# Eight row scatters per block: one burst, or one per round behind the newest matmul

## The chip, the cores and the metric

The kernel runs on one core of one Trainium2 chip. The metric is the device time of one execution in microseconds. The kernel before was run three times without the profiler: 1150.1, 1150.43 and 1151.41 us, so the median is 1150.43 us. One more execution was recorded by the profiler. A core has four compute engines with a queue of instructions each: PE (matrix multiply), DVE (vector), ACT (activations), POOL (GpSimd); SP only issues DMAs here. Each queue is worked off in order, and engines wait for each other through semaphores.

## The reference, cut to what matters

A pre-norm block over 4 sequences of 2048 tokens, width 256, float32: causal linear attention with 16 heads, then a mixture of 8 experts, two experts for each token.

```
x = x + linear_attention(layernorm(x))        # elu(q)+1, elu(k)+1, running sums over the sequence
h = layernorm(x)
logits = h @ router_w.T                       # 8 experts
top2, idx = top_k(logits, 2); p = softmax(top2)
x = x + sum over the two experts e of p_e * (gelu(h @ w1[e] + b1[e]) @ w2[e] + b2[e])
```

The reference works out every expert for every token and weights with zeros. The kernel computes only the chosen pairs, so it has to sort tokens by expert: that is what the scatters are for.

## The kernel before, in words

The 8192 tokens are 16 blocks of 512. A block passes through three stages in three successive steps of the outer loop (line 907): `stage_a` (norm, q, k, v, prefix sums), `stage_b` (scores and values, 128 tokens at a time) and `stage_c` (output projection, second norm, router, places of the tokens). In step s the loop runs `stage_a(s)`, `stage_b(s - 1)` and `stage_c(s - 2)` side by side. They are Python generators: one round of the inner loop (lines 926 to 933) advances each of them to its next `yield`, which writes its instructions down.

`stage_c` ends with the routing: DVE works out for each of the 512 tokens, and for each of its two experts, a row number in a table `rows` in DRAM in which each expert has a region (`slots`, line 616). Then eight indirect DMAs on POOL's queue (line 620; two experts by four groups of 128 tokens) write the normalised token with its weights there, one row of 1040 bytes per token. Before the change all eight are written down in one piece of `stage_c`, in its fourth round, so they stand one behind the other in POOL's queue.

The expert part works on tiles of 256 rows of one expert (`slot_tiles`, line 728; 68 tiles). SP fetches the rows of a tile three tiles ahead (`fetch_rows`, line 734), first-layer weights two ahead (`fetch_in`), second-layer weights and bias one ahead (`fetch_out`). A fetch of rows waits for every scatter written down so far (`after(i, writes + cleared)`, line 747). PE transposes the rows (`turned`, line 776), multiplies by the first weights (`hidden`, ph, line 804), ACT applies gelu (line 810), PE multiplies by the second weights (`output`, py, line 821), DVE adds bias and weights the rows (y, lines 826 and 830), and two indirect DMAs on POOL add the tile to the output (`store`, line 835), each pair after the pair before it has landed. Tiles can be worked on while later blocks are still in attention: as soon as a round of tiles is known to be full (`ROUND_ENDS`), the inner loop mixes steps of that work (two per tile) between the rounds of the stages. How early in a step they come is set by one number per kind of step:

```
order = (20, 12, 5)[(s > NBLK - 1) + (s > NBLK)]
...
        i += 1
        while ran < share and ran * order < i * share:
            work.step()
            ran += 1
```

A planner of the framework then orders each engine's list; only SP's is kept as written. POOL has, besides scatters and adds, one addition of the output bias per block (`x`, line 319).

Of the kernel before, what the change touches and what calls it, by code (L numbers as in the profile page):

```python
# [24 lines left out]
def kernel(  # L25
# [41 lines left out]
    nc = tc.nc  # L67
# [241 lines left out]

    made = {}  # L310
    zlast = [None]

    entered = {}

# [9 lines left out]
    def stage_a(n: int):  # L324
        b, s0 = blocks[n]
        if n not in entered:
            enter(n)
            yield
        xt, xn = entered.pop(n)
        if n + 1 < len(blocks):  # L330
            xs[n + 1] = load_x(n + 1)
        xnT = att.tile([P, NCC, TB], F32, tag="xnT", name=f"xnT_{n}")
        transposed(xn, xnT, "xn")
        yield
        qT = att.tile([P, NCC, TB], F32, tag="qT", name=f"qT_{n}")
        kT = att.tile([P, NCC, TB], F32, tag="kT", bufs=2, name=f"kT_{n}")
        for w, bias, dst in ((wk_sb, bk_sb, kT), (wq_sb, bq_sb, qT)):
            for m in range(NCC):
                pp = bank([P, TB], "pp")
                for cc in range(NCC):  # L340
                    nc.tensor.matmul(  # L341
                        pp, w[:, cc, ts(m, P)], xnT[:, cc, :],
                        start=(cc == 0), stop=(cc == NCC - 1),
                    )
                elu1(pp, bias[:, m : m + 1], dst[:, m, :])
            yield

        z = att.tile([P, NCC, TB], F32, tag="z", name=f"z_{n}")
        carry = small.tile([P, NCC], F32, tag="carry", name=f"carry_{n}")
        for m in range(NCC):  # L350
            nc.vector.tensor_tensor_scan(
                z[:, m, :], kT[:, m, :], kT[:, m, :],
                0.0 if s0 == 0 else zlast[0][:, m : m + 1], ALU.add, ALU.bypass,
            )
        nc.vector.tensor_copy(carry, z[:, :, TB - 1])
        zlast[0] = carry
        nc.vector.tensor_tensor(z, z, qT, ALU.mult)
        vp = vpads[n % 2]
        vp_v = vp.rearrange("p t q (s d) -> p t q s d", s=4)[:, :, :, 0::3, :]
        for t2 in range(NT // 2):  # L360
            pv = bank([P, 2, D], "pv")
            for j in range(2):
                for cc in range(NCC):
                    nc.tensor.matmul(  # L364
                        pv[:, j, :], xnT[:, cc, ts(2 * t2 + j, P)], wv_sb[:, cc, :],
                        start=(cc == 0), stop=(cc == NCC - 1),
                    )
            for j in range(2):
                nc.vector.tensor_tensor(
                    vp_v[:, 2 * t2 + j],  # L370
                    pv[:, j, :].rearrange("p (q s d) -> p q s d", s=2, d=HD),
                    bv_bc.rearrange("p (q s d) -> p q s d", s=2, d=HD),
                    ALU.add,
                )
        yield
        k_tok = att.tile([P, NT, D], F32, tag="k_tok", bufs=2, name=f"k_tok_{n}")
        for t2 in range(NT // 2):
            pk = bank([P, 2, D], "pk")
            for j in range(2):
                for m in range(NCC):  # L380
                    nc.tensor.transpose(  # L381
                        pk[:, j, ts(m, P)], kT[:, m, ts(2 * t2 + j, P)], ident
                    )
            nc.scalar.copy(k_tok[:, 2 * t2 : 2 * t2 + 2, :], pk)
        if n < ROUND_ENDS[0] + 2:

            enter(n + 1)
        yield

        pd = bank([P, P], "pd")  # L390
        for m in range(NCC):
            for t in range(NT):
                nc.tensor.matmul(
                    pd[W * t : W * t + W, :], heads[:, m, :], z[:, m, ts(t, P)],
                    start=(m == 0), stop=(m == NCC - 1), skip_group_check=True,
                    tile_position=(0, W * t),
                )
        rden = small.tile([P, P], F32, tag="rden", name="rden")
        nc.vector.tensor_scalar_add(rden, pd, DEN_EPS)
        nc.vector.reciprocal(rden, rden)  # L400
        yield
        qs = att.tile([P, NCC, TB], F32, tag="qs", bufs=2, name=f"qs_{n}")
        prs = [bank([P, NCC, P], f"pr_{t}") for t in range(NT)]
        for m in range(NCC):
            for t in range(NT):
                part = slice(W * t, W * t + W)
                nc.tensor.matmul(
                    prs[t][:, m, :], spread[part, m], rden[part, :], start=True, stop=True,
                    tile_position=(W * t, 0),
                )  # L410
        for t in range(NT):
            nc.vector.tensor_tensor(
                qs[:, :, ts(t, P)], qT[:, :, ts(t, P)], prs[t], ALU.mult
            )
        made[n] = (xt, kT, qs, k_tok, vp, vp_v)
        yield
# [4 lines left out]
    def stage_b(n: int):  # L421
# [35 lines left out]
        for c in range(NT):  # L457
            nxt = scores(c + 1) if c + 1 < NT else None
            yield
            st = sstate[0]  # L460
            pn = bank([P, NCC, P], "pn")
            for m in range(NCC):
                for g in range(NG):
                    part = slice(W * g, W * g + W)
                    nc.tensor.matmul(  # L465
                        pn[part, m, :], st[part, m], qs[part, m, ts(c, P)],
                        start=(m == 0), stop=False, skip_group_check=True,
                        tile_position=(W * g, W * g),
                    )
            for m in range(NCC):  # L470
                for par in range(2):
                    for g in range(NG):
                        nc.tensor.matmul(  # L473
                            pn[W * g : W * g + W, m, :],
                            vp[:, c, NG * m + g, W * par : W * par + W],
                            at[:, g, m, par, :],
                            start=False, stop=(par == 1), skip_group_check=True,
                            tile_position=(0, W * g),
                        )
            nc.scalar.copy(vT[:, :, ts(c, P)], pn)  # L480
            if s0 + (c + 1) * P < S:
                for m in range(NCC):
                    for g in range(NG):
                        nc.tensor.matmul(
                            state_ps[W * g : W * g + W, m],
                            k_tok[:, c, P * m + W * g : P * m + W * g + W],
                            vp_v[:, c, NG * m + g],
                            start=(s0 == 0 and c == 0 and m == 0), stop=True,
                            skip_group_check=True, tile_position=(0, W * g),
                        )  # L490
                st = small.tile([P, NCC, 2, HD], F32, tag="S", bufs=2, name=f"S_{n}_{c}")
                nc.vector.tensor_tensor(
                    st, state_ps, own2.unsqueeze(1).to_broadcast([P, NCC, 2, HD]), ALU.mult
                )
                sstate[0] = st
            at = nxt
            yield
# [13 lines left out]
    def stage_c(n: int):  # L511
# [103 lines left out]
        slots = small.tile([P, M], U32, tag="slots", name="slots")  # L615
        nc.vector.tensor_copy(slots, slot_f)
        nc.vector.tensor_copy(ends[:, :, 0], upto[:, :, M])
        for k in range(2):
            for t in range(NT):
                s = ins_of(nc.gpsimd.indirect_dma_start(  # L620
                    out=rows[:, :],
                    out_offset=bass.IndirectOffsetOnAxis(
# [3 lines left out]
                ))  # L626
                apart(s, "rows")
                after(s, cleared)
                writes.append(s)
        yield  # L630

# [96 lines left out]
    def slot_tiles(todo):  # L728
# [67 lines left out]
        def hidden(j):  # L796
            xT, w1t, bias = (state[j][key] for key in ("xs", "w1", "bias"))
            hT = moe.tile([P, NFC, ST], F32, tag="hT", name="hT")
            for f2 in range(NFC // 2):
                ph = bank([P, 2, ST], "ph")  # L800
                for i in range(2):
                    f = 2 * f2 + i
                    for cc in range(NCC):
                        nc.tensor.matmul(  # L804
                            ph[:, i, :], w1t[:, cc, ts(f, P)], xT[:, cc, :],
                            start=(cc == 0), stop=(cc == NCC - 1),
                        )
                for i in range(2):
                    f = 2 * f2 + i
                    nc.scalar.activation(  # L810
# [4 lines left out]
        def output(j):  # L815
# [2 lines left out]
            py = bank([P, NS, D], "py")  # L818
            for a in range(NS):
                for f in range(NFC):  # L820
                    nc.tensor.matmul(  # L821
                        py[:, a, :], hT[:, f, ts(a, P)], w2t[:, f, :],
                        start=(f == 0), stop=(f == NFC - 1),
                    )
            yt = moe.tile([P, NS, D], F32, tag="y", bufs=4, name=f"y_{j}")
            nc.vector.tensor_tensor(  # L826
                yt, py, b2t.unsqueeze(1).to_broadcast([P, NS, D]), ALU.add
# [79 lines left out]
    for s in range(NBLK + 2):  # L907
# [13 lines left out]
            left = max(0, left - 2 * HOLD)  # L921
        share = -(-left // (upto - s + 1))
        ran = 0
        order = (20, 12, 5)[(s > NBLK - 1) + (s > NBLK)]
        i = 0
        while gens:
            for it in list(gens):
# [64 lines left out]
```

## Time and profile before

| | us |
|---|---|
| median of three runs | 1150.43 |
| the profiled execution, its own time | 1243.11 |
| its span, first to last instruction | 1241.1 |
| PE busy in the span | 1088.4 |
| DVE busy | 750.7 |
| ACT busy | 414.0 |
| POOL busy | 389.1 |
| mean granted PE clock, share of full speed | 0.931 |

The profiled execution takes 92.7 us more than the median of the runs without the profiler. In a row of groups the columns are line, engine, operation, what it writes and reads, count, then busy time and the mean of one, then the engine's idle time ahead of them and who ended it. In a row of the timeline they are start, duration, engine, line, operation, names, count, and in brackets the idle time of the engine and what ended it; "issue" means that the profile shows nothing that the engine waited for, and "remote" that the release came with no recorded instruction at its time. In a table by windows each row gives a stretch, its length, and for each engine the busy time and the number of instructions, then the granted PE clock, the share of the DMA engines and GB/s.

By stretches the span divides so: up to 70 us the start; to about 225 us blocks in attention alone; to 420 us the first expert tiles among them; from 420 to 898 us seven steps of the loop that look alike, with four tiles each; to about 1020 us the last two steps; then 25 tiles alone until PE ends at 1217.4 us; and 23.7 us in which the last output adds land.

### The profile page before, as it was taken

Reading aid. Unit: us, or ns where it says so; the run is one execution under the profiler, and the core shown is the slowest. Engines: PE = TensorE matmul, PEld = TensorE weight load, DVE = VectorE, ACT = ScalarE, POOL = GpSimd, SP = SyncE. Lnnn points to the kernel's source line nnn. Section 1 sums busy time; section 2 is a strip of 40 time slices with the busy share of each in tenths; the row PEclk is TensorE's granted clock in tenths of the full one; section 3 lists DMA queues with packets and bytes.
Section 4 is the critical chain, followed back from the end, with each engine's and each line's share of the span. In section 5 each row is a group of like instructions: output and inputs, shape, how many; then the busy total and the mean of one; then the engine's idle time right before and its main releaser. Section 6 shows DMA issues by size and latency. Waiting matters only on the chain.

```text
span 1241.1 us, 25308 instructions
## 1 busy us (share of the span) xinstructions
PE 1088.4 (88%) x9504; PEld 835.7 (67%) x9504; DVE 750.7 (60%) x2535; ACT 414.0 (33%) x824; POOL 389.1 (31%) x302
## 2 busy tenths in 40 slices
PE   4987777888888999899998999998999969999992
PEld 2655544565757677676776776776768748888881
DVE  8775856667576857675674848674676455333330
ACT  3442322424242525344352625253343112222220
POOL 4002113021313342324233242423242424444444
PEclk9888877888888999999998999899999979999996
DMA  5011111523323446172636364451726348898873
GB/s 188 2 35 41 42 51 42 162 92 81 112 69 112 124 107 184 50 214 63 195 76 184 95 169 122 123 151 46 202 62 184 96 133 258 234 232 229 238 169 39
DMA packets 128732, 155.37 MB, mean 125 GB/s; under 512 B 9952, under 2 KB 105952, under 8 KB 128608
## 3 DMA queue, kind: packets, MB, share of 16 engines
q1 hardware_dynamic: 84944, 101.78, 26.1%
q0 software_dynamic: 25728, 34.88, 15.3%
q10 hardware_dynamic: 17936, 17.07, 4.3%
q8 instruction: 76, 1.25, 0.4%
q14 instruction: 48, 0.39, 0.1%
HBM read 108.05 MB, written 45.65 MB: 124 GB/s over the span
## 4 chain that ended last, share of the span: by engine, by line
PE 67%; DVE 23%; issue 4%; DMA 2%; another core or an unknown queue 2%; ACT 1%; ACTq 0%; POOL 0%; DVEq 0%; POOLq 0%
PE py L821 19%; PE ph L804 16%; PE pp L341 7%; PE pn L473 6%; DVE at L447 5%; DVE st L269 3%; PE pv L364 3%; PE pn L465 3%; PE sc L442 3%; PE pt_xn L262 2%; DMA out_dram<-y,to 2%; PE pt_xs L776 2%; DVE x L524 2%; PE pk L381 1%
## 5 line engine op out<-in xcount | busy, mean ns | idle before, releaser
L835 POOL DMA_INDIRECT out_dram<-y,to x136 | 217.6, 1600 | 513.2 <-DVE y L830 329.4
L821 PE MATMUL py<-w,hT 128*128 128x256 f32 x1088 | 263.3, 395 | 4.8 <-issue 4.8
L804 PE MATMUL ph<-xT,w 128*128 128x256 f32 x1088 | 254.0, 386 | 2.2 <-issue 1.4
L821 PEld LDWEIGHTS py<-w,hT 128*128 128x128 f32 x1088 | 209.5, 198 | 44.4 <-issue 15.6
L804 PEld LDWEIGHTS ph<-xT,w 128*128 128x128 f32 x1088 | 207.6, 193 | 33.9 <-issue 4.4
L810 ACT ACTIVATE hT<-ph,b1t 128x256 f32<-128x256 f32 x272 | 114.0, 470 | 344.2 <-PE ph L804 288.7
L447 DVE TENSOR_TENSOR at<-sc,causal 128x512 f32<-128x512 f32 x256 | 160.4, 683 | 21.0 <-PE sc L442 14.9
L826 DVE TENSOR_TENSOR y<-py,b 128x512 f32<-128x512 f32 x68 | 47.0, 690 | 197.7 <-PE py L821 186.7
L620 POOL DMA_INDIRECT rows<-xn,slots x128 | 124.2, 970 | 84.8 <-issue 83.0
L777 DVE COPY xT<-pt_xs 128x512 f32<-128x512 f32 x68 | 46.9, 690 | 120.5 <-PE pt_xs L776 97.1
L319 POOL TENSOR_TENSOR x<-x,bo_bc 128x1024 f32<-128x1024 f32 x16 | 39.2, 2449 | 248.0 <-ACT xn L293 97.8
L473 PE MATMUL pn<-at,vpad 128*32 128x128 f32 x2048 | 92.3, 301 | 15.7 <-issue 15.3
L473 PEld LDWEIGHTS pn<-at,vpad 128*32 128x32 f32 x2048 | 62.7, 119 | 37.7 <-issue 36.9
L433 ACT ACTIVATE qM<-qs,parity 128x256 f32<-128x256 f32 x128 | 57.0, 499 | 91.5 <-issue 35.2
L262 PE MATMUL pt_xn<-ident,xn 128*128 128x128 f32 x256 | 47.3, 328 | 44.8 <-DVE xn L298 43.4
L480 ACT COPY vT<-pn 128x256 f32<-128x256 f32 x64 | 23.6, 368 | 176.2 <-PE pn L473 84.9
L442 PE MATMUL sc<-qM,kT 32*128 32x256 f32 x1024 | 75.7, 405 | 0.7 <-DVE xT L777 0.7
L262 PEld LDWEIGHTS pt_xn<-ident,xn 128*128 128x128 f32 x256 | 35.7, 168 | 56.9 <-issue 34.6
L442 PEld LDWEIGHTS sc<-qM,kT 32*128 32x128 f32 x1024 | 47.5, 187 | 27.1 <-issue 17.5
L341 PE MATMUL pp<-xnT,wq_sb 128*128 128x512 f32 x128 | 62.3, 627 | 0.0
L341 PE MATMUL pp<-xnT,wk_sb 128*128 128x512 f32 x128 | 59.8, 611 | 0.2 <-ACT xnT L263 0.2
L519 PE MATMUL px<-wo_sb,vT 128*128 128x256 f32 x256 | 59.4, 385 | 0.0
(152 smaller groups left out, 1375.2 us busy)
## 6 DMA issues: line engine op xcount, KB each, us to landing
w<-in_w_dram SPq DMA_DIRECT2D x136, 512.0 KB
xs<-rows SPq DMA_DIRECT2D x68, 260.0 KB
b<-in_b_dram SPq DMA_DIRECT2D x68, 128.0 KB
out_dram<-x ACTq DMA_DIRECT2D x16, 512.0 KB
x<-in_x_dram ACTq DMA_DIRECT2D x15, 512.0 KB
rows<-none SPq DMA_DIRECT2D x1, 2340.0 KB
out_dram<-y,to POOLq DMA_INDIRECT x136
rows<-xn,slots POOLq DMA_INDIRECT x128
```

Of the source, the lines that this page charges most:

```text
L262: nc.tensor.transpose(pt[:, t, :], src[:, t, ts(cc, P)], ident)
L341: nc.tensor.matmul(pp, w[:, cc, ts(m, P)], xnT[:, cc, :], start=(cc == 0), stop=(cc == NCC - 1),)
L433: nc.scalar.activation(qM[:, :, par, :], qs[:, :, ts(c, P)], AF.Copy, scale=parity[:, par : par + 1],)
L442: nc.tensor.matmul(sc[g][:, m, :, :], kT[part, m, ts(c, P)], qM[part, m, :, :], start=True, stop=True,)
L447: nc.vector.tensor_tensor(at[:, g].rearrange("p m r i -> p (m r) i"), sc[g].rearrange("p m r i -> p (m r) i"), causal.unsqueeze(1).to_broa ...
L473: nc.tensor.matmul(pn[W * g : W * g + W, m, :], vp[:, c, NG * m + g, W * par : W * par + W], at[:, g, m, par, :], start=False, stop=(par = ...
L519: nc.tensor.matmul(px[:, j, :], vT[:, cc, ts(2 * t2 + j, P)], wo_sb[:, cc, :], start=(cc == 0), stop=(cc == NCC - 1),)
L620: s = ins_of(nc.gpsimd.indirect_dma_start(out=rows[:, :], out_offset=bass.IndirectOffsetOnAxis(ap=slots[:, 2 * t + k : 2 * t + k + 1], axi ...
L804: nc.tensor.matmul(ph[:, i, :], w1t[:, cc, ts(f, P)], xT[:, cc, :], start=(cc == 0), stop=(cc == NCC - 1),)
L810: nc.scalar.activation(hT[:, f, :], ph[:, i, :], AF.Gelu, bias=bias[:, f : f + 1])
L821: nc.tensor.matmul(py[:, a, :], hT[:, f, ts(a, P)], w2t[:, f, :], start=(f == 0), stop=(f == NFC - 1),)
L835: i = ins_of(nc.gpsimd.indirect_dma_start(out=out_rows, in_=yt[:, a, :], in_offset=None, compute_op=ALU.add, bounds_check=T - 1, oob_is_er ...
```

## The change

Block n's scatters are spread over rounds: from the second on, each is preceded by a `yield` of `stage_c`, and each of the eight is made to wait on a semaphore for the matmul that was written down last among those of six places: pk, pd, pn of the attention, ph and py of the tiles, each now passed through `issued`. The last block keeps its scatters together. `stage_c` has seven rounds more for that, and `order` is raised from 20 to 27 and from 12 to 19 for the steps concerned.

```
+    latest = []
+
+    def issued(i):
+        latest[:] = [ins_of(i)]
...
-                        nc.tensor.matmul(
+                        issued(nc.tensor.matmul(
                             pn[W * g : W * g + W, m, :],
...
-                        )
+                        ))
...
+        spread_out = n < len(blocks) - 1
         for k in range(2):
             for t in range(NT):
+                if spread_out and (k or t):
+                    yield
                 s = ins_of(nc.gpsimd.indirect_dma_start(
...
                 apart(s, "rows")
                 after(s, cleared)
+                if spread_out:
+                    after(s, latest)
                 writes.append(s)
...
-        order = (20, 12, 5)[(s > NBLK - 1) + (s > NBLK)]
+        order = (27, 19, 5)[(s > NBLK - 1) + (s > NBLK)]
```

The same wrapping in `issued` is made at pk (line 381), pd (393), ph (804) and py (821).

More of the change, by code (lines that the diff above doesn't have):

```diff
@@ L380, in stage_a @@
                 for m in range(NCC):
-                    nc.tensor.transpose(
+                    issued(nc.tensor.transpose(
                         pk[:, j, ts(m, P)], kT[:, m, ts(2 * t2 + j, P)], ident
-                    )
+                    ))
             nc.scalar.copy(k_tok[:, 2 * t2 : 2 * t2 + 2, :], pk)
@@ L396, in stage_a @@
                     tile_position=(0, W * t),
-                )
+                ))
         rden = small.tile([P, P], F32, tag="rden", name="rden")
@@ L472, in stage_b @@
                     for g in range(NG):
-                        nc.tensor.matmul(
+                        issued(nc.tensor.matmul(
                             pn[W * g : W * g + W, m, :],
@@ L478, in stage_b @@
                             tile_position=(0, W * g),
-                        )
+                        ))
             nc.scalar.copy(vT[:, :, ts(c, P)], pn)
@@ L803, in hidden @@
                     for cc in range(NCC):
-                        nc.tensor.matmul(
+                        issued(nc.tensor.matmul(
                             ph[:, i, :], w1t[:, cc, ts(f, P)], xT[:, cc, :],
                             start=(cc == 0), stop=(cc == NCC - 1),
-                        )
+                        ))
                 for i in range(2):
@@ L820, in output @@
                 for f in range(NFC):
-                    nc.tensor.matmul(
+                    issued(nc.tensor.matmul(
                         py[:, a, :], hT[:, f, ts(a, P)], w2t[:, f, :],
                         start=(f == 0), stop=(f == NFC - 1),
-                    )
+                    ))
             yt = moe.tile([P, NS, D], F32, tag="y", bufs=4, name=f"y_{j}")
```

## The prediction

> **What bounds the kernel now.** I read the page first, for the span, the engines and the scatters' group.
>
> ```profile
> span 1241.1 us, 25308 instructions
> ...
> PE 1088.4 (88%) x9504; PEld 835.7 (67%) x9504; DVE 750.7 (60%) x2535; ACT 414.0 (33%) x824; POOL 389.1 (31%) x302
> ...
> L620 POOL DMA_INDIRECT rows<-xn,slots x128 | 124.2, 970 | 84.8 <-issue 83.0
> ```
>
> PE is the bound; POOL is busy for 31% and the chain of waits gives it 0%. So the change can pay only where scatters hold up PE. The windows of one of the seven like steps (the part ahead of block 10's eight scatters, the scatters, the part behind) show whether they do:
>
> ```profile
> 693.89:718.63 24.74, 24.48 (x197) 17.68 (x196) 18.01 (x51) 12.11 (x20) 8.93 (x5) 1.00 0.24 44
> 718.63:729.97 11.34, 8.94 (x79) 5.93 (x78) 1.05 (x4) 1.44 (x4) 7.71 (x8) 1.00 0.36 108
> 729.97:760.68 30.71, 29.63 (x300) 24.06 (x300) 23.04 (x83) 13.69 (x30) 6.92 (x5) 1.00 0.77 219
> ```
>
> PE (first pair) is full ahead and behind, and idles 2.4 of 11.34 us during the scatters. The timeline of PE shows that it loses more than idle time:
>
> ```profile
> 721.02 1.47 PE L473 MATMUL pn<-at,vpad 128*32 128x128 f32 x31
> 722.84 0.27 PE L473 MATMUL pn<-at,vpad 128*32 128x128 f32 x1 [0.35 <-issue]
> 723.04 0.82 PE L381 MATMUL pk<-ident,kT 128*128 128x128 f32 x4
> 724.31 0.54 PE L381 MATMUL pk<-ident,kT 128*128 128x128 f32 x3 [0.45 <-issue]
> 725.02 0.27 PE L381 MATMUL pk<-ident,kT 128*128 128x128 f32 x1 [0.17 <-issue]
> 725.73 1.12 PE L821 MATMUL py<-w,hT 128*128 128x256 f32 x4 [0.45 <-issue]
> 727.15 1.24 PE L821 MATMUL py<-w,hT 128*128 128x256 f32 x5 [0.30 <-issue]
> 728.59 0.91 PE L821 MATMUL py<-w,hT 128*128 128x256 f32 x3 [0.20 <-issue]
> 730.00 1.02 PE L821 MATMUL py<-w,hT 128*128 128x256 f32 x4 [0.50 <-issue]
> 730.96 0.50 PE L442 MATMUL sc<-qM,kT 32*128 32x256 f32 x4
> ```
>
> From start to next start, pn takes 2.02 us, pk 2.69, py 5.23, with pauses for which the profile names no cause. Undisturbed, the same groups look like this (the step of block 8's scatters):
>
> ```profile
> 599.92 1.08 PE L473 MATMUL pn<-at,vpad 128*32 128x128 f32 x32
> 600.82 0.31 PE L484 MATMUL state_ps<-vpad,k_tok 128*32 128x32 f32 x16
> ...
> 603.41 3.72 PE L821 MATMUL py<-w,hT 128*128 128x256 f32 x16
> 607.07 1.15 PE L442 MATMUL sc<-qM,kT 32*128 32x256 f32 x16
> ```
>
> There pn takes 0.90 and py 3.66; pk's eight transposes take about 0.96, as eight of the same shape (pt_xn) do. So this burst costs PE 1.1 + 1.7 + 1.6 = 4.4 us. Last, who waits:
>
> ```profile
> ACT vT L480 <- remote: 81.2, 9, 9.4
> ...
> SPq L743 <- DMA rows<-xn,slots: 125.0, 16, 49.5
> ```
>
> Nine times ACT's copy of pn starts up to 9.4 us after pn's last record, when a burst ends[...].
>
> **The change part by part.**
>
> *The bursts removed.* I summed PE's time beyond the undisturbed time of what it ran, from first scatter to 1.5 us after the last, over all sixteen bursts: 91 us; 73 us if each window is set against one of equal length ahead of it (early blocks wait on DVE anyway). If that were all real it would be 6 to 8% of the median. But these numbers belong to a recorded execution, and that one takes 1243.11 us, 92.7 more than the median of 1150.43. The 92.7 us have to lie somewhere in this trace. They are not in the 25 tiles at the end (PE busy 173.00 of the 173 us from 1038 on), nor in the like steps outside bursts (PE is busy 64.35 of 68.4 us on the mean of six of them, and the rest lies mostly in the bursts). Taking the bursts out gives 1243 - 91 = 1152, almost the median. Nothing else of that size is there.
>
> [...] in the burst of block 15 (from 1019.71 us, the same eight scatters) PE runs only the long ph and py and loses at most 1.5 us; in the other bursts it has just sent pn, 32 matmuls in 0.9 us. [...] By the rows alone the burst is worth 73 to 91 us[...]. I take 0 us and keep 0 to -75 (15 of 16 bursts change) as ends.
>
> *The clock.* [...] In the burst at 581.19 the granted clock falls to 0.5 for 3.4 us[...]. But py takes 5.33 us there, and 5.23 us in the burst above at clock 1.00: the measurement decides, and the clock is charged nothing of its own.
>
> *The waits.* 120 scatters wait for a matmul. It is older in the program than anything queued behind them: in POOL's list of the changed kernel, from block 6 on, the order is 2 scatters, adds of a tile, 3 scatters, adds, 3 scatters, adds, then the bias addition. An add needs a later py, so it would have waited anyway; four y buffers and 12 to 17 us per tile cover some us of lateness. The bias addition is needed two steps later. Cost 0; without that cover, a late add would hold DVE's y, then PE.
>
> *SP.* Its list is unchanged, but fetches of rows now wait for two or three scatters, several times per step, not once for eight. Today one such fetch stands until 593.15 us, right after a burst; its rows are transposed near 615, and the first-layer weights queued behind it (593.72) are used at 611.70: 18 us of cover. A group of three scatters is 3.8 us of POOL plus landing. Cost 0 while a fetch is held less than about 15 us longer than today.
>
> *The number 27.* This moves work on every engine. Instruction counts are equal but for ACT, with 14 table loads less (1.28 us each, 18 us, off the path: ACT is busy 33%). PE's list has the same instructions in another order from block 5 on. In the like steps, tiles' ph and py now stand one by one between short attention groups. I followed each short group to what it waits for. Undisturbed there is little to win: per step sc to pt_xn2 stands 1.0 us for the second norm and 0.4 us in pt_xn2; plt 0.3. In the changed order PE has the same work between px and pt_xn2, but DVE's norm no longer has a tile's copy (0.69 us) and small operations in front: perhaps 0.5 to 1 us per step. Near the end, ph 41 moves between pn and px, where PE stood 1.2 us. Against it: in block 5's step only sc (1.1 us) now lies between pd and pr, whose reciprocal needs about 1.3 us, and the router's pc of two steps lies 4.6 us behind plt, not 8. Ten steps at -0.6, -1 at the end, +1 early: -6 us, bounds +3 and -10.
>
> Sum against the recorded execution: 1243 less 55 to 75 us of bursts, about 1170 to 1185. Against the median: 1150.4 - 6 = 1144.5.
>
> **The rivals.**
>
> *The bursts are real without the profiler as well* (12%). For it: nothing in the trace names the recorder. Against: the 92.7 us would then need another home. A quarter of the 75 us gives about 1130, all 1075.
>
> *Nothing gained from the order* (13%): the norm chain stands just as long, about 1150.
>
> *Slower, through SP* (28%): a fetch of rows waits for scatters that wait for a matmul that waits for DVE; behind it the weights of the next tile queue up. It decides when a fetch is held over 15 us longer than today; beyond that each us late is a us of PE. The 49.5 us longest wait of that kind speaks for it, the 18 us of cover against. One us in each of ten steps, without the gain of the order: 1160; half of it, 1155.
>
> **How the numbers follow.** Likeliest (47%) is the order's gain alone: 1144.5, its own range 1141 to 1149. What a measurement of this kernel can tell from no change is about 0.2%, 2.3 us. Of the 47%, 9 end within that; with the 13% of the second rival, same is 22%; faster 38 + 12 = 50%; slower 28%. The range leaves out the lower half of the first rival and the far end of the third: 1124 to 1160.
>
> **What would show it.** Right: the recorded execution falls by 55 us or more while the median moves by less than 1%; pn, pk and py near scatters back at 0.9, 1.0 and 3.6 us; "remote" gone from ACT's waits; PE full in the steps. Wrong: a median 20 us or more lower (the bursts were real), or SP's waits on scatters grown with PE waiting for ph or pt_xs (the third rival). If single scatters still stop PE, the recorded execution hardly falls.

## The result and the profile after

The changed kernel takes 1183.88 us (median of 6 runs, 1175.12 to 1191.05) against 1150.92 us (6 runs, 1150.1 to 1152.77) for the kernel before: 1.028 times as long, 95% interval 1.0258 to 1.0301. The prediction was 1144.5 us, 1124 to 1160: wrong in sign, and outside its range. The profiled execution of after is its fastest, 1175.12 us. Its page, with the span, the busy times and the scatters' group:

```profile
span 1173.4 us, 25336 instructions
...
PE 1046.8 (89%) x9504; PEld 810.5 (69%) x9504; DVE 752.6 (64%) x2535; ACT 395.2 (34%) x810; POOL 386.5 (33%) x302
...
L628 POOL DMA_INDIRECT rows<-xn,slots x128 | 125.5, 980 | 299.7 <-PE pv L368 87.2
```

POOL's idle time ahead of the scatters has grown from 84.8 to 299.7 us and is now owed mostly to PE (226.8 us of it): the change does what it says. PE's busy time must not be set against the 1088.4 us of before, which belong to an execution of 1243 us. A second recorded execution of the kernel before (experiment 1) is the one to compare with: span 1148.3 us, PE busy 1035.8.

The timeline of PE around the second group of state products (`state_ps`) in a like step shows where the time goes. After:

```profile
442.04 0.31 PE L488 MATMUL state_ps<-vpad,k_tok 128*32 128x32 f32 x16
442.17 0.62 PE L539 MATMUL pl<-xn2T,rw_sb 128*32 128x128 f32 x16
446.33 0.33 PE L488 MATMUL state_ps<-vpad,k_tok 128*32 128x32 f32 x16 [3.55 <-DVE S L496]
```

The same place in the second execution of before:

```profile
446.89 0.31 PE L484 MATMUL state_ps<-vpad,k_tok 128*32 128x32 f32 x16
447.13 3.72 PE L804 MATMUL ph<-xT,w 128*128 128x256 f32 x16
450.69 0.60 PE L776 MATMUL pt_xs<-ident,xs 128*128 128x128 f32 x4
451.22 0.64 PE L535 MATMUL pl<-xn2T,rw_sb 128*32 128x128 f32 x16
451.68 0.31 PE L484 MATMUL state_ps<-vpad,k_tok 128*32 128x32 f32 x16
```

Both groups write the one state tile in PSUM, so the second may start only when DVE has read the first (S, line 496). Before, 4 us of a tile's `ph` and `pt_xs` lay between them; after, only `pl` does, 0.6 us, and PE stands 3.55 us.

Behind some stands of this kind PE also ran at a lower granted clock, which the second recorded execution of after (experiment 5) shows best. The timeline of PE behind a stand in a like step, then the stretch of `pp` by windows:

```profile
450.12 0.44 PE L488 MATMUL state_ps<-vpad,k_tok 128*32 128x32 f32 x16 [4.27 <-DVE S L496]
450.75 5.85 PE L345 MATMUL pp<-xnT,wq_sb 128*128 128x512 f32 x8
456.54 1.15 PE L446 MATMUL sc<-qM,kT 32*128 32x256 f32 x16
...
450.75:456.54 5.79, 5.79 (x10) 2.21 (x9) 3.26 (x18) 1.36 (x3) 2.32 (x2) 0.61 0.44 61
```

The same in the second execution of before:

```profile
452.41 3.60 PE L341 MATMUL pp<-xnT,wq_sb 128*128 128x512 f32 x8
455.94 1.15 PE L442 MATMUL sc<-qM,kT 32*128 32x256 f32 x16
...
452.41:455.94 3.53, 3.53 (x9) 1.34 (x8) 2.69 (x17) 2.35 (x3) 0.00 (x0) 1.00 0.00 0
```

From start to next start `pp` takes 5.79 us at a mean granted clock of 0.61, and 3.53 us at 1.00: time multiplied by clock is 3.53 in both. PE is not idle ahead of `sc`; it runs part of `pp` at a granted clock of 0.50. In all seven like steps of that execution of after `pp` takes 5.23 to 6.19 us, in those of before 3.53.

The chain of waits of after, followed back from the stand of 3.55 us, names what S itself was late for:

```profile
427.60 7.32 DMA out_dram<-x
...
435.07 0.38 ACTq L116
...
435.55 1.09 ACT xn L293 x2
...
441.73 1.28 DVE z L355
...
444.83 0.67 DVE y L836
...
445.57 0.57 DVE y L840 x2
446.15 0.14 DVE S L496
...
446.33 0.33 PE state_ps L488 x16
```

Read it from the bottom. S stands on DVE behind a tile's `y` (lines 836 and 840) and the scan of the keys (355). The scan is late because ACT is late: ACT's list holds the load of the next x (line 116), and that load waits for the store of the block's residual (line 550), issued by ACT at 427.60, which takes 7.32 us to land. So there are two causes in one stand: an order (y ahead of S, nothing long to cover it), and a wait (store, load, ACT, DVE). The experiments take them apart; the slower clock came on top, an estimated 17.4 us in the like steps of the second execution.

To say where time goes I use one table. "Lost" is PE's time from the start of one group of matmuls to the next, less the undisturbed duration of the group's matmuls, summed by stretch over the profiled execution. Steps are turns of the outer loop from 0, each counted from its last router product `pl` to the next step's; 8 to 14 are the seven like steps. Of what is lost in these, "stands" is PE's idle time ahead of the state products, and "half clock" is half of PE's busy time at a granted clock of 0.50, an estimate of what it would have saved at 1.00. The early column hangs on where its first step is cut, by up to some 2.7 us.

| kernel | median us | lost, steps 5 to 7 | lost, steps 8 to 14 | of it stands | of it half clock | lost, last stretch |
|---|---|---|---|---|---|---|
| before (second execution) | 1149.37 | 41.7 | 23.2 | 0.0 | 0.0 | 18.7 |
| after (second run) | 1185.41 | 35.0 | 61.0 | 25.8 | 17.4 | 26.6 |
| spreading and waits, old placing | 1148.86 | 39.4 | 23.7 | 0.4 | 0.0 | 18.4 |
| placing alone | 1166.25 | 34.6 | 36.6 | 13.3 | 5.1 | 26.5 |
| after with 28 | 1167.81 | 42.4 | 30.7 | 8.6 | 1.7 | 27.2 |
| after, loads of x tied | 1160.58 | 34.4 | 33.1 | 12.2 | 1.7 | 26.4 |
| with 28, loads of x tied | 1159.04 | 45.5 | 21.4 | 0.0 | 0.0 | 24.9 |
| late placing in steps 0 to 7 only | 1143.88 | 36.0 | 23.7 | 0.0 | 0.0 | 18.5 |

From before to after the three columns of lost time add up to +37.8 in the like steps, +7.9 at the end and -6.7 early, 39.0 us; the spans of the two executions, 1186.8 and 1148.3 us, differ by 38.5. At the end, too, part is the clock: half clock costs PE 8.1 us there in after and 3.5 in before, by the same estimate.

### The profile page after: what moved, and what is told of

Read it like the earlier page. It is cut to its first block, busy times and chain, and to the rows that moved or that the text cites. A ratio compares the mean times of both kernels' runs of the same rounds, so it can differ in the third digit from the quotient of the medians.

```text
span 1173.4 us, 25336 instructions
## 1 busy us (share of the span) xinstructions
PE 1046.8 (89%) x9504; PEld 810.5 (69%) x9504; DVE 752.6 (64%) x2535; ACT 395.2 (34%) x810; POOL 386.5 (33%) x302
## 4 chain that ended last, share of the span: by engine, by line
PE 62%; DVE 25%; DMA 6%; ACT 4%; issue 2%; ACTq 0%; POOL 0%; DVEq 0%; POOLq 0%; SPq 0%
PE ph L814 17%; PE py L831 17%; PE pp L345 6%; DVE at L451 6%; PE pn L477 4%; PE pv L368 3%; DVE st L269 3%; PE sc L446 3%; DMA out_dram<-y,to 2%; PE pn L469 2%; PE pt_xs L786 2%; DMA out_dram<-x 2%; PE pt_xn L262 2%; DVE x L528 2%; DVE z L355 1%
## 5 line engine op out<-in xcount | busy, mean ns | idle before, releaser
L845 POOL DMA_INDIRECT out_dram<-y,to x136 | 214.4, 1577 | 267.1 <-DVE y L840 95.0
L831 PE MATMUL py<-w,hT 128*128 128x256 f32 x1088 | 251.8, 385 | 0.0
L814 PE MATMUL ph<-xT,w 128*128 128x256 f32 x1088 | 251.0, 384 | 0.5 <-DVE xT L787 0.5
L814 PEld LDWEIGHTS ph<-xT,w 128*128 128x128 f32 x1088 | 204.6, 191 | 36.0 <-issue 4.0
L831 PEld LDWEIGHTS py<-w,hT 128*128 128x128 f32 x1088 | 204.0, 192 | 33.1 <-issue 4.9
L628 POOL DMA_INDIRECT rows<-xn,slots x128 | 125.5, 980 | 299.7 <-PE pv L368 87.2
L820 ACT ACTIVATE hT<-ph,b1t 128x256 f32<-128x256 f32 x272 | 114.2, 469 | 226.8 <-PE ph L814 221.9
L262 PEld LDWEIGHTS pt_xn<-ident,xn 128*128 128x128 f32 x256 | 34.6, 163 | 57.3 <-issue 47.2
L477 PE MATMUL pn<-at,vpad 128*32 128x128 f32 x2048 | 72.5, 285 | 0.0
L345 PE MATMUL pp<-xnT,wq_sb 128*128 128x512 f32 x128 | 70.3, 694 | 0.0
L477 PEld LDWEIGHTS pn<-at,vpad 128*32 128x32 f32 x2048 | 54.3, 113 | 13.8 <-issue 13.4
L345 PE MATMUL pp<-xnT,wk_sb 128*128 128x512 f32 x128 | 63.5, 639 | 0.2 <-ACT xnT L263 0.2
L484 ACT COPY vT<-pn 128x256 f32<-128x256 f32 x64 | 23.7, 370 | 113.9 <-PE pn L477 113.8
```

The costliest lines, as they stand in the source:

```text
L262: nc.tensor.transpose(pt[:, t, :], src[:, t, ts(cc, P)], ident)
L345: nc.tensor.matmul(pp, w[:, cc, ts(m, P)], xnT[:, cc, :], start=(cc == 0), stop=(cc == NCC - 1),)
L477: issued(nc.tensor.matmul(pn[W * g : W * g + W, m, :], vp[:, c, NG * m + g, W * par : W * par + W], at[:, g, m, par, :], start=False, stop ...
L628: s = ins_of(nc.gpsimd.indirect_dma_start(out=rows[:, :], out_offset=bass.IndirectOffsetOnAxis(ap=slots[:, 2 * t + k : 2 * t + k + 1], axi ...
L814: issued(nc.tensor.matmul(ph[:, i, :], w1t[:, cc, ts(f, P)], xT[:, cc, :], start=(cc == 0), stop=(cc == NCC - 1),))
L820: nc.scalar.activation(hT[:, f, :], ph[:, i, :], AF.Gelu, bias=bias[:, f : f + 1])
```

## The experiments

Twelve runs follow, two of them of the kernels before and after again; ratios are against the kernel before, timed beside each on the same chip. The first four were to tell apart three theories: P, the loss comes from the placing of the tiles' work (the number 27); W, it comes from the waits of the scatters and of what follows them; R, the pauses of before belong to the recording. Two more came after those four: S, the store, is stated ahead of experiment 5, and its rival D ahead of experiment 6. "Tied" below means tied by order of issue.

**1. Before, again.** No edit.

> The kernel before, unchanged, once more. If the pauses of PE in the bursts belong to full recording (theory R), its recorded execution again takes about 1243 us and the others 1150. If they come and go by themselves, the recorded execution is sometimes near 1150, or some of the others near 1243.

1149.37 us, ratio 0.999 (0.9978 to 1.0003); profiled execution 1150.21 us. Its timeline of PE during block 9's eight scatters (POOL has them from 591.75 to 601.74):

```profile
593.97 1.08 PE L473 MATMUL pn<-at,vpad 128*32 128x128 f32 x32
594.98 1.09 PE L381 MATMUL pk<-ident,kT 128*128 128x128 f32 x8
595.91 3.62 PE L821 MATMUL py<-w,hT 128*128 128x256 f32 x16
599.46 1.15 PE L442 MATMUL sc<-qM,kT 32*128 32x256 f32 x16
```

pn, pk and py take 1.01, 0.93 and 3.55 us: no pauses, recorded as before, with the same eight scatters in a row. So neither the scatters nor the recording as such makes the pauses; they were a trait of that one execution. What caused them there stays open.

**2. The spreading and its waits without the new placing.** The rounds that the spreading adds are not counted, and the order numbers are the old ones; PE, DVE, ACT and SP then run the same lists as before; from block 6 on POOL has three scatters, the adds of a tile, then five.

```
-                    yield
+                    yield "scatter"
...
-        order = (27, 19, 5)[(s > NBLK - 1) + (s > NBLK)]
+        order = (20, 12, 5)[(s > NBLK - 1) + (s > NBLK)]
...
+                if what == "scatter":
+                    extra += 1
+                if not (extra > 2 and it is c_gen):
+                    i += 1
```

> Scatters spread and waiting for matmuls as in the change, but the tiles' steps placed where the kernel before has them: the lists of PE, DVE, ACT and SP are those of before, entry by entry, and only POOL's differs (groups of three and five scatters instead of eight). Theory P (placing): the loss of 33 us comes from the tiles' steps moved by the 27; this kernel then takes what before takes, 1145 to 1153 us, and the 3.1 us stand of PE between pl and state_ps is gone. Theory W (waits): the loss comes from scatters that wait for matmuls and from fetches of rows that wait for scatters; this kernel is then slow as well, 1170 us or more. Theory R (recorder): the bursts cost only while the profiler records in full; its recorded execution is then within 1% of its own median, with no burst pauses of more than some 2 us.

1148.86 us, ratio 0.9988 (0.9977 to 0.9999). Spread and waiting scatters cost nothing where the tiles stand as before, though fetches leave late here too: the last four ahead of the store of a like step start 4.7 to 1.5 us before it, in after (first execution) 3.3 to 0.4, in the second execution of before 8.3 to 4.3. The loads of x leave 6.0 to 8.1 us after the store, in before 6.0, and PE hardly stands for it. (The sum of SP's waits for scatters does not tell the kernels apart: 456.5 us here, 459.2 in after, 438.3 in the second execution of before.) W alone falls.

**3. The placing without spreading or waits.** The kernel before with seven empty `yield`s in `stage_c` and the numbers 27 and 19: PE, DVE, ACT and SP run the lists of after, the scatters stand eight together.

```
+        if n < len(blocks) - 1:
+            for _ in range(7):
+                yield
         yield
...
-        order = (20, 12, 5)[(s > NBLK - 1) + (s > NBLK)]
+        order = (27, 19, 5)[(s > NBLK - 1) + (s > NBLK)]
```

> The tiles' steps placed as in the changed kernel (seven empty rounds, 27 and 19), but the eight scatters together and without waits: the lists of PE, DVE, ACT and SP are those of the changed kernel, only POOL's differs. Theory P: 1175 to 1190 us by the median, as the changed kernel. Theory W: about 1145 to 1155 us. Theory R: the recorded execution is 60 to 90 us above the median of this kernel, because the bursts of eight are back.

1166.25 us, ratio 1.0148 (1.0116 to 1.018). The placing alone costs 16 us; the table puts 13.4 of them in the like steps and 7.8 at the end, 7.1 being won in steps 5 to 7. But neither part alone gives the 33 us: some 18 come only from both together.

**4. The order number 28 in place of 27**, all else as after. It puts `py` behind the first state products, so S stands ahead of `y` on DVE.

```
-        order = (27, 19, 5)[(s > NBLK - 1) + (s > NBLK)]
+        order = (28, 19, 5)[(s > NBLK - 1) + (s > NBLK)]
```

> The changed kernel with one number altered, 28 for 27 in the like steps. In PE's list the py behind pp now comes after pn and state_ps, and in DVE's list S comes ahead of the tile's y, so that state_ps need not wait for y. Theory P, with the stand of 3.1 us in each of about ten steps as its place: 25 to 32 us less than the changed kernel, 1150 to 1158 us. If the placing costs in another place or in several, only a part comes back: 1165 to 1180. Theory W: no difference, about 1184 us.

1167.81 us, ratio 1.0163 (1.0138 to 1.0187). About half of the loss comes back.

**5. After, again**, to see whether the 18 us are the chip's.

> The kernel after, unchanged, for a second reading beside the next three. With the placing alone the time had been 1166.25 us, with placing and waits together 1183.88, though PE, DVE, ACT and SP run the same lists in both: some 18 us come only when the scatters also wait. Theory S (store): because the scatters end later, SP's fetch of a half tile's rows and the weights queued behind it are issued some 8 us later in the step, just when ACT issues the store of the block's residual; the store then lands 6.9 to 8.4 us after its issue, against 3.3 to 4.2 with the placing alone; ACT's next load of x into the same buffer waits for it, everything behind on ACT (normalised rows, exp of the keys) is late, then DVE's scan, then S, then PE. By S this run repeats: 1175 to 1191 us, and stores of 6.5 us and more in the profile. Theory C (chip): the 18 us belong to the chip or the day of that measurement; then this run takes about 1166.

1185.41 us, ratio 1.0294 (1.0264 to 1.0324). They are the kernel's. How theory S came about is seen by setting the two kernels' SP beside each other: the four transfers that the work on one tile issues for later tiles (rows, two weights, bias: 260, 512, 512 and 128 KB), in the timeline of SP of after:

```profile
425.24 0.37 SPq L753 DMA_DIRECT2D xs<-rows  x1
425.82 0.37 SPq L765 DMA_DIRECT2D w<-in_w_dram  x1
426.44 0.37 SPq L773 DMA_DIRECT2D w<-in_w_dram  x1
427.04 0.35 SPq L777 DMA_DIRECT2D b<-in_b_dram  x1
```

and with the placing alone, whose step stands 1.36 us later in the trace:

```profile
418.76 0.37 SPq L746 DMA_DIRECT2D xs<-rows  x1
419.32 0.37 SPq L758 DMA_DIRECT2D w<-in_w_dram  x1
422.77 0.37 SPq L766 DMA_DIRECT2D w<-in_w_dram  x1
423.50 0.35 SPq L770 DMA_DIRECT2D b<-in_b_dram  x1
```

In after the last scatter leaves 17 us later in the step (21.9 us ahead of the step's last router product `pl`, against 39.3), the fetch of rows waits for them, and all four transfers start in the 2.4 us ahead of ACT's store at 427.60. With the placing alone they are spread over 5 us and start 5 to 10 us before the store (428.96). Where the traces have the landings, the stores of the like steps take 3.3 to 4.2 us with the placing alone and 6.9 to 8.3 us in the two executions of after. POOL's adds to the output lie alike in both (the last two 4.4 and 2.4 us ahead of this store, 4.1 and 2.2 with the placing alone), so they are not the difference. With the placing alone each load of x leaves 5.3 us after its store, and does not wait for it. In after the last stores have no load behind them, since all of x has been read: the first of these (758.19 in the first execution, 771.84 in the second) takes 7.06 and 7.34 us, and PE stands only 1.94 us behind it, as with the placing alone; behind the six stores with a load it stands 2.1 to 3.9 us in the first execution and 3.4 to 4.5 in the second.

**6. Five buffers for x**, two for the second normalised rows.

```
-        xt = att.tile([P, NT, D], F32, tag="x", bufs=4, name=f"x_{n}")
+        xt = att.tile([P, NT, D], F32, tag="x", bufs=5, name=f"x_{n}")
...
-        xn2 = att.tile([P, NT, R], F32, tag="xn2", bufs=3, name=f"xn2_{n}")
+        xn2 = att.tile([P, NT, R], F32, tag="xn2", bufs=2, name=f"xn2_{n}")
```

> The kernel after with five buffers for x in place of four, and two for the second normalised rows in place of three to make room. PE, POOL and SP run the same lists; on ACT the loads of x stand at the same places but each brings the block that is one later, into a buffer whose store was issued a whole step before. So nothing on ACT waits for the store just issued. By theory S the 18 us go and the placing's 16 stay: about 1166 us, 1162 to 1172, with the stand of PE ahead of the second group of state products back at about 2 us in the like steps. By a rival D (DVE and POOL disturb one another while the scatters run, or the fetches of rows themselves hold PE) nothing changes: 1180 to 1190.

1183.73 us, ratio 1.0285 (1.0247 to 1.0323): nothing gained, as rival D had it. But the edit did not do what I wrote. The scheduler moved each load one step forward, and it still waited for the store just issued: in the trace a store lands 60.99 us after step 9's last `pl`, the mark from which I count, and the load leaves at 61.14. The run decides nothing about S.

**7. The same buffers in the kernel before.**

> The control: the kernel before with the same buffers as e7. In its like steps the load of x is issued 6 us after the store, when the store has landed in 3.4 to 5.9 us, so both theories expect no change: 1148 to 1152 us. A gain here would mean that e7's edit helps for another reason than the store.

1151.05 us, ratio 1.0009 (1.0 to 1.0019): no gain.

**8. 28 and five buffers.**

> The order number 28 (S ahead of y on DVE again) and five buffers for x together, waits kept. By theories P and S the two repairs are for different delays in front of the same product, so the like steps should come down to nearly those of before (62.5 us, from 63.4 on average with 28 alone) while the last stretch of 320 us against 308 stays as it is: about 1160 us, 1156 to 1165. If S is wrong: 1166 to 1169, as with 28 alone.

1166.3 us, ratio 1.0136 (1.0112 to 1.016): at the number given for "S is wrong", but with the same flaw as 6: a store lands 58.70 us after step 11's mark, its load leaves at 58.86.

**9. After, with the loads of x tied** behind the store of four blocks before, and the buffers of experiment 6 (five for x, two for the second normalised rows).

```
-            nc.scalar.dma_start(
+            d = nc.scalar.dma_start(
...
+            if n >= 4: tc.add_manual_dep(ins_of(d), stored[n - 4].name, mybir.DependencyInfo(mybir.DependencyClass.NoSync, mybir.DependencyReason.SCHED_ONLY), reason="order of issue")
```

> With five buffers alone the scheduler had simply moved every load of x one step forward, so that it still waited for the store just issued (in its trace a store landed at 60.99 us after the step's mark and the load left at 61.14): that run left theory S untested. Here each load is also tied by order behind the store of four blocks before, so it stands two or three ACT instructions behind the store just issued, but its buffer was emptied by the store of the step before. PE, DVE and POOL run the same lists as after. By S the stand of PE ahead of the second group of state products falls from 3.1 to 4.5 us to the 2 us of the placing alone, and the time from 1184 to 1166 (1162 to 1172). By D (DVE and POOL in each other's way, or the fetches of rows themselves) it stays at 1180 to 1190.

1160.58 us, ratio 1.0095 (1.0074 to 1.0117): 23 to 25 us less than after, 1.4 us under the range that I gave. The timeline of ACT around the store at the end of step 8:

```profile
424.42 0.39 ACTq L551 DMA_DIRECT2D out_dram<-x  x1
...
425.63 0.38 ACTq L116 DMA_DIRECT2D x<-in_x_dram  x1
...
430.76 1.09 ACT L294 ACTIVATE xn<-x,shift,guess 128x256 f32<-128x256 f32 x2 [0.31 <-DVE shift L289]
```

The load leaves 1.2 us after the store, and ACT's normalised rows now wait 0.31 us for DVE instead of following a load. The stores still take 7.3 to 8.4 us to land, so it was the wait for them that cost, not the traffic itself, and the SP fetches, as late as in after, hold nothing up: D falls. What is left in front of the state products is 1.6 to 1.9 us in each like step: the placing's part. With the stands shorter the half clock goes as well, 1.7 us against 17.4.

**10. 28, with the loads tied.**

> The same on top of the number 28, waits kept. With 28 PE stood 1.3 to 2.6 us in the like steps ahead of the same products; by S this was the late load of x too, and goes: like steps of 62 to 62.5 us and a time of 1158 to 1162, the last stretch still 320 us against 308. If the fetches themselves hold PE: 1166 to 1168 as before the edit.

1159.04 us, ratio 1.0089 (1.0066 to 1.0112), as expected. The like steps lose 21.4 us, less than in the kernel before (23.2): both causes are out of them, with spreading and waits still in. No stand ahead of the state products is left and no half clock. The rest of the difference lies in the last stretch (24.9 against 18.7) and the early steps (45.5 against 41.7).

**11. The tied loads in the kernel before.**

> The control for the two runs with the tied loads: the same edit (five buffers for x, loads tied behind the store of four blocks before) in the kernel before, whose loads of x had 6 us to spare behind the store. By S it gains nothing here: 1147 to 1152 us, like steps of 62.3 to 62.5 us. If the edit helps by itself (it also moves two of ACT's instructions), it would take some 5 us or more off here too, and the 23 us that it took off after would not all be the store's.

1150.66 us, ratio 1.0005 (0.9992 to 1.0017): the edit gains nothing where the load had 6 us to spare.

**12. The late placing for the first eight steps only**, spreading and waits kept. The edit against experiment 2:

```
-        order = (20, 12, 5)[(s > NBLK - 1) + (s > NBLK)]
+        order = (27 if s < 8 else 20, 12, 5)[(s > NBLK - 1) + (s > NBLK)]
...
-                if not (extra > 2 and it is c_gen):
+                if s < 8 or not (extra > 2 and it is c_gen):
```

> The spreading and its waits with the placing of after only in the first eight steps and the placing of before from there on. The late placing saved 3 to 5 us of PE's standing in the sixth step (19.2 us of lost time against 22.4 to 24.2) and cost only in the later ones. Theory P: 1143 to 1147 us, a little under both kernels. If the placing of the early steps only pushes the same standing to later: 1148 to 1152.

1143.88 us, ratio 0.9949 (0.9931 to 0.9967): faster than both kernels, by little but clear of the interval. Against spreading and waits with the old placing, from which it differs only in the first eight steps, the table has the gain in steps 5 to 7 (36.0 us lost against 39.4), with the later stretches as before.

## Why the prediction was wrong, step by step

*The bursts removed: 0 us.* The number held: before, recorded again, has no pauses to remove, and spreading alone (experiment 2) moves the median by 0.1%. That the pauses come from the recording was my estimate, and it was not shown: the second recorded execution of the same program, with the same bursts, has none. The sign promised for it, a recorded execution 55 us and more below 1243, came true (1175.12) and proves nothing: before, recorded again, takes 1150.21. The 9.4 us that I gave for ACT's copies of pn are ACT's idle time; the nine copies start 5.7 to 7.0 us after pn's last record, and the trace does not show what released them. Ninety-three microseconds between one profiled execution and the median should have asked for a second one before anything else.

*The clock: nothing.* This step failed. The mean granted clock is 0.960 in the second execution of before, 0.954 and 0.942 in the two of after; half clock costs PE 0, 8.4 and 17.4 us in their like steps (the table's estimate), where it runs through `pp` behind the new stands. The comparison by which the prediction set the clock aside was misread. This is the `py` of 5.33 us in the burst at 581.19:

```profile
588.28 5.40 PE L821 MATMUL py<-w,hT 128*128 128x256 f32 x16 [0.45 <-issue]
```

It runs in one piece; 3.1 us of it lie in the stretch at 0.5, and 3.66 us undisturbed and half of 3.1 make 5.2. The `py` of 5.23 us at clock 1.00 is broken by pauses. Two causes gave about the same time by chance. Nor does the clock follow the length of a stand alone: in the second execution of after all six stands of 3.4 to 4.5 us have 6.8 us at 0.50 beside them, but in the first those of 3.08 and 3.55 us have none and one of 1.94 us has 3.4. That fits the scatter of after's times: its two runs with the lowest mean clock, 0.943, took 1184.93 and 1191.05 us, the two with the highest, 0.954 and 0.956, took 1175.12 and 1176.73.

*The waits: 0.* Right for POOL itself, by experiment 2.

*SP: 0 while a fetch is held less than 15 us longer.* This step failed, by 18 us with the half clock that came with it. Its cover was worked out for the users of what is fetched, and that cover held: PE's stands in the like steps lie ahead of the state products (and 0.3 us ahead of pt_xn), not ahead of `pt_xs`, `ph` or `py`. What I left out is who else uses the DMA engines at the new time, and who waits for that: the store of the residual, then the load of x into its buffer, then everything behind that load in ACT's list. The link from load to stand is shown (experiment 9, with 11 as its control, and the store without a load); that the store is slow because of the bunched fetches is read from the traces and was not tried by itself. With the old placing fetches nearly as late cost nothing. The 125.0 us of waits for scatters belong to the disturbed execution; the second one of before has 438.3. The third rival, slower through SP at 28%, had the sign, but it ran through PE waiting for `ph` or `pt_xs`, which did not come.

*The number 27: -6, bounds +3 and -10.* This step failed: experiment 3 gives +16, where -6 was put down. "I followed each short group to what it waits for" was done for the groups that stood before, and on PE's list; I did not ask what each short group would wait for once its long neighbour had left, nor look at how DVE's list moved. The tile's step that ran between the two groups now stands earlier, as `py` ahead of pn. That takes both the cover between the two groups of state products and, through `y`, the place of S on DVE. The chain of dependence (one PSUM tile, written twice, read once between) is in the code; DVE's new order was to be had before any run. The gain by the norm chain did come: PE's stand ahead of that pt_xn falls from 1.0 to 0.3 us in each like step. But the new stands outweigh it. The early cost that I gave as +1 is a gain instead, about 7 us in steps 5 to 7. The router's pc, named as a risk, is part of the loss at the end: PE stands 3.78 us there ahead of one pc in after, 0.44 us in the second execution of before and in experiment 12.

Sum: 1150 + 16 (placing) + 18 (the wait for the store and the half clock with it, only with that placing) = 1184; measured 1183.88 and 1185.41. The 18 is the difference of after and experiment 3. In the like steps of the two traces 24.4 us lie between them, about half of it stands (25.8 against 13.3) and half of it half clock (17.4 against 5.1). Experiment 9 ends 5.7 us below experiment 3; in the like steps 3.5 us of that show, and half clock accounts for 3.4 of them (5.1 against 1.7). The recorded execution of after was to be about 1170 to 1185; 1243 less 55 to 75 is 1168 to 1188.

## What to carry to other kernels

When work is moved between short operations, ask of every short operation what covered its wait before and whether that cover still stands next to it, on the list of each engine that feeds it and not only on the busiest one. When a transfer is made later, look past its own users. In after, ACT's list held a DMA issue that waited for another transfer to land (the store of 7.32 us), and ACT stood 2.29 us ahead of the normalised rows behind it. With that load tied to a buffer that had long been free ACT stood 0.31 us there, and the time was 1160.58 us against 1183.88 and 1185.41: look for such issues. Where a stand has been added, look also at the granted clock behind it: in the like steps of after it cost an estimated 17.4 us, beside stands of 25.8. And record a second execution before explaining what a first one shows beyond the median.

## What the runs showed of the hardware

A 512 KB store took 3.3 to 4.2 us in the like steps of the placing alone, and 6.9 to 8.4 us in those of after and of experiment 9, where 1412 KB of fetches start between 3.3 us ahead of it and 0.7 us behind it. In after, fetches and store together, 1924 KB from 425.24 to 434.92 us, moved at an estimated 204 GB/s; with all else that moved, the windows give 234 GB/s for that stretch, the DMA engines busy for 0.91 of it, and the page's slices at the end give 233 and 234 as well. Eight 128x512 products that take 3.53 us at a granted clock of 1.00 took 5.79 us at a mean of 0.61; the stretches at 0.50 lasted 3.4 or 6.8 us in the like steps, and beside PE's stands of 1.9 us they came in some steps and not in others (three of seven with the placing alone). One recorded execution of an unchanged program showed pauses of PE at its scatters and took 1243.11 us, where the next took 1150.21.
